# Row additions of two layer norms and the closing addition as accumulating transfers, with the closing norm in place

## The chip, the cores and the metric

The kernel runs on one core of a Trainium2 chip. The engines of the core are PE (matrix products), DVE (vector), ACT (activations), POOL (GpSimd) and SP, which here only issues transfers; each runs its own instructions in order and waits on semaphores for the others. The metric is the device time of one execution in microseconds.

## The reference, cut to what matters

The input x has 8 batches of 2048 nodes with 256 features; adj is a 2048 x 2048 mask. Two graph layers follow one another, each with a residual and a layer norm around it. Layer 0 is an attention over chunks of 256 nodes with four heads of 64:

```
scores = clip(q k / 8, -10, 10); where adj == 0: -10
attn   = softmax(scores) within each chunk of 256 nodes
ctx    = sum over the 8 chunks of attn v
out    = layernorm(ctx Wo + bo + x) * gamma + beta
x1     = layernorm(x + out)
```

Layer 1 is a graph attention on x1, again with four heads:

```
Wh    = x1 W
e     = leaky_relu(s_src + s_dst), masked by adj
alpha = softmax(e)
h     = elu(alpha Wh)
result = layernorm(x1 + h)
```

## The kernel before, in words

Everything is in float32 but the masks. The 2048 nodes of a batch are cut into four groups of 512 (four tiles of 128 rows). The loop over batches b runs layer 0 of batch b, and beside it layer 1 of batch b-1, and the closing norm of batch b-2. Layer 0 has 64 slots (4 groups of queries x 2 pairs of heads x 8 chunks), taken as 32 pairs; the loop `for p in range(PAIRS)` (L1104) emits one pair. With q = p // 8 and i = p % 8, pair p belongs to group q.

In each pair PE makes the scores `ps` (L398) of the next pair in four units, DVE clips them into `pr` (L415), ACT takes exponents in place (L438), PE multiplies with the values into `pc` (L449), ACT copies `pc` to `raw` (L456), DVE takes the reciprocal of the row sums (L466), and POOL scales and adds to `acc` (L473, L475). Beside it, `along` is layer 1 of the batch before: DVE makes four tiles `e` per pair from a row, a column and the mask `et` (L842), and PE multiplies each into `pa` (L871). When a head of layer 1 is done for eight tiles of rows, `close` (L891) divides, applies the elu and writes the result into `h1` in its last step on DVE (L915). The first such write of a batch falls into pair 6 and fills one head of rows 0 to 7 of `h1`.

All engines follow an order written out by hand: what is emitted first stands first in the queue of its engine. Transfers are issued by SP (loads, stores) and ACT (stores of `acc` and of x1). What stands in the list `outgoing` is sent at the start of the next pair by `send` (L205).

The work between the layers is done for one group at a time by class `Between` (L573), in steps that are hooked into the pairs by tables. For group q-1 during group q: `xg` is loaded at i=0 (L579), `bias` adds bo at i=2 (L584), PE makes the output projection `po` at the ends of i=2 and 3, `add` (L611) forms y at the starts of i=3 and 4, ACT takes sums and squares at the ends of i=4 and 5, `shift` (L588) adds beta - bo to `xg` at i=6, and ACT applies the norm at the end of i=6. In the group after that, `scale` (L617) multiplies with gamma at i=0, `again` (L620) adds `xg` at i=1, and the second norm follows: sums at the end of i=1, squares at i=2, then the apply and the store of x1. The last group of a batch is done between the batches by the list `steps` (L1232), and the last-but-one finishes at the last pair (L1187) and in the list `early`; these call the same methods.

The closing norm of batch b-2 is class `Close` (L930) driven by the table `CLOSING` (L1055): for each group g it loads x1 from `x1D` into `x1g` (L943), adds it to `h1` on DVE (L946), lets ACT take sums and squares, and writes the normed rows into `x1g` (L951), from which SP stores them (L952). Batches 6 and 7 have their closing norm after the loop over pairs, by the tables `CLOSING_ALONE` and `ENDING`; there POOL does the addition and the rows go through free space in `kT` and `qT`.

Of the kernel before, what the change touches and what calls it, by code (L numbers as in the profile page):

```python
# [8 lines left out]
F32 = mybir.dt.float32  # L9
# [4 lines left out]
ALU = mybir.AluOpType  # L14
AX = mybir.AxisListType

P = 128
# [4 lines left out]
def adj_resnorm_kernel(  # L22
# [19 lines left out]
    nc = tc.nc  # L42
    B, N, F = x.shape
    H, D = a_src.shape
    NT = N // P
    NCH = N // CH
# [8 lines left out]
    QT = CH // P  # L55
# [32 lines left out]
    blocks = ctx.enter_context(tc.tile_pool(name="blocks", bufs=2))  # L88
# [30 lines left out]
    qT = big.tile([P, KC, N], F32, tag="qT", name="qT")  # L119
    kT = big.tile([P, KC, N], F32, tag="kT", name="kT")  # L120
# [6 lines left out]
    x1D = tc.dram_tile([B, N, F], F32, name="x1D")  # L127
# [18 lines left out]
    def row(ap, name):  # L146
        t = consts.tile([P, F], F32, tag=name, name=name)
        nc.scalar.dma_start(out=t, in_=ap.partition_broadcast(P))
        return t
# [8 lines left out]
    bo_sb = row(bo, "bo_sb")  # L158
    gamma_sb = row(gamma, "gamma_sb")
    beta_sb = row(beta, "beta_sb")  # L160
# [44 lines left out]
    def send():  # L205
        while outgoing:
            outgoing.pop(0)()


    class Masks:  # L210
# [3 lines left out]
        def __init__(self):  # L214
            self.pieces = [
                (QT * q + u, m) for q in range(NCH) for m in range(len(PIECES)) for u in range(QT)
            ]
            self.raw, self.bits, self.done = [], [], []
            self.next = 0
# [47 lines left out]
    def by_node(dram, b, g):  # L267

        return dram[b, g * CH : (g + 1) * CH, :].rearrange("(t p) f -> p t f", p=P)
# [45 lines left out]
    def project(b, g):  # L315
# [18 lines left out]
        def linear(dst, w, bias, apart=False):  # L334
            if apart:
                pps = [one_bank([P, CH], "pp") for _ in range(KC)]
            else:
                pp = two_banks([P, KC, CH], "pp")
                pps = [pp[:, c, :] for c in range(KC)]
            for c in range(KC):  # L340
                for kc in range(KC):
                    nc.tensor.matmul(  # L342
                        pps[c],
                        lhsT=w[:, kc, c * P : (c + 1) * P],
                        rhs=st["xT"][:, kc, :],
                        start=(kc == 0),
                        stop=(kc == KC - 1),
                    )
            for c in range(KC):
                nc.scalar.activation(  # L350
                    dst[:, c, cols], pps[c], AF.Identity, bias=bias[:, c : c + 1]
                )
# [83 lines left out]
    def exps(s, u):  # L436
        pr = probs[s][u]
        nc.scalar.activation(pr, pr, AF.Exp, scale=0.125)  # L438
# [38 lines left out]
    sums = {}  # L477
# [95 lines left out]
    class Between:  # L573
# [5 lines left out]
            self.r = load_x(b, g, "xg")  # L579
            self.y = blocks.tile([P, QT, F], F32, tag="y", name="y")  # L580

        def bias(self):
            row = bo_sb.unsqueeze(1).to_broadcast([P, QT, F])
            nc.vector.tensor_add(self.r, self.r, row)  # L584

        def shift(self):
            row = beta_sb.unsqueeze(1).to_broadcast([P, QT, F])
            nc.vector.tensor_add(self.r, self.r, row)  # L588

        def output(self, us, parts=HALVES):  # L590
            n = len(us)
# [17 lines left out]
        def add(self, us):  # L609
            here = slice(us[0], us[0] + len(us))  # L610
            nc.vector.tensor_add(self.y[:, here, :], self.po, self.r[:, here, :])  # L611
            if us[0] == 0:
                self.a = Norm(self.y, "a")
# [2 lines left out]
            row = gamma_sb.unsqueeze(1).to_broadcast([P, QT, F])  # L616
            nc.vector.tensor_mul(self.y, self.y, row)  # L617

        def again(self):
            nc.vector.tensor_add(self.y, self.y, self.r)  # L620
            self.b2 = Norm(self.y, "b")

        def finish(self):
# [38 lines left out]
        4: lambda o: o.add((2, 3)),  # L662
    }
    MIDDLE_OF = {
        2: lambda o: o.bias(),
        6: lambda o: (o.a.factors(), o.shift()),
    }
    FINALLY_OF = {
        4: lambda o: o.a.sums(every),
# [6 lines left out]
    }  # L676
    NEXT_MIDDLE = {
        0: lambda o: o.scale(),
        1: lambda o: o.again(),
        3: lambda o: o.b2.factors(),  # L680
        4: lambda o: o.load(),
        5: lambda o: o.turn(),
# [4 lines left out]
        3: lambda o: o.finish(),  # L687
    }
    NEXT_LAST = {
        5: lambda o: o.values((0, 1)),  # L690
        6: lambda o: o.values((2, 3)),
    }
# [237 lines left out]
    class Close:  # L930


        def __init__(self, b, g, home):
            self.b, self.g = b, g
            self.h = h1[:, QT * g : QT * (g + 1), :]
            if len(home) == 3:
                pool, tag, bufs = home
                self.x = pool.tile([P, QT, F], F32, tag=tag, name="x1g", bufs=bufs)
            else:
                room, k = home  # L940
                at = k % 2 * QT * F
                self.x = room[:, k // 2, at : at + QT * F].rearrange("p (t f) -> p t f", f=F)
            nc.sync.dma_start(out=self.x, in_=by_node(x1D, b, g))  # L943

        def add(self, engine=nc.vector):
            engine.tensor_add(self.h, self.h, self.x)  # L946
            self.n = Norm(self.h, "c")

        def finish(self):
# [38 lines left out]
                else:  # L988
                    nc.scalar.activation(dst, src, AF.Identity, bias=off, scale=rs)

    HOME = (blocks, "xb", 2)
    HOME_Y = (blocks, "y", 2)

    class Closing:

# [4 lines left out]
        def do(self, s, *kinds):  # L1000
            for g, step, *more in self.table.get(s, ()):
                if step not in kinds:
                    continue
                if step == "load":
                    self.of[g] = Close(self.b, g, more if len(more) > 1 else more[0])
                elif step == "finish":
                    self.of[g].finish()
                elif step == "add":
                    self.of[g].add()
                elif step == "pool":  # L1010
                    self.of[g].add(nc.gpsimd)
                elif step == "stats":
                    self.of[g].n.stats((0, 1, 2, 3))
                elif step == "most":
                    self.of[g].add_most()
                elif step == "sums":
                    self.of[g].n.sums((0, 1, 2, 3))
                elif step == "squares":
                    self.of[g].n.squares((0, 1, 2, 3))
                elif step == "factors":  # L1020
                    self.of[g].n.factors()
# [9 lines left out]
    for g in range(NCH):  # L1031
# [21 lines left out]
            finish_constants()  # L1053

    CLOSING = {  # L1055
        -1: [(0, "load", HOME), (1, "load", HOME)],
        0: [(0, "add"), (0, "sums")],
        1: [(0, "squares")],
        2: [(1, "add"), (0, "factors"), (0, "finish"), (2, "load", HOME_Y)],
        3: [(1, "sums")],  # L1060
        4: [(1, "squares"), (3, "load", HOME_Y)],
        5: [(2, "add"), (1, "factors"), (1, "finish")],
        6: [(2, "sums")],
        7: [(2, "squares")],
        8: [(3, "add"), (2, "factors"), (2, "finish")],
        9: [(3, "sums")],
        10: [(3, "squares")],
        11: [(3, "factors"), (3, "finish")],
    }
    CLOSING_ALONE = {  # L1070
        -1: [(g, "load", kT, g) for g in range(NCH)],
        1: [(0, "pool")],
        2: [(1, "pool")],
        3: [(0, "stats")],
        4: [(1, "stats")],
        5: [(0, "finish")],
        6: [(1, "finish")],
        8: [(2, "pool")],
        9: [(3, "pool")],
        10: [(2, "stats")],  # L1080
        11: [(3, "stats")],
        12: [(2, "finish")],
        13: [(3, "finish")],
    }
    ENDING = {
        30: [(g, "load", qT, g) for g in range(NCH)],
        37: [(0, "pool")],
        38: [(1, "pool")],
        39: [(0, "stats")],
        40: [(1, "stats")],  # L1090
        41: [(0, "finish")],
# [5 lines left out]
    for b in range(B):  # L1097
        waug = blocks.tile([P, NT, H, D1], F32, tag="waug", name="waug")
        sd = small.tile([P, 2 * H, NT], F32, tag="sd", name="sd", bufs=1)
        closing = Closing(b - 2, CLOSING) if b > 1 else None  # L1100
        if closing:
            closing.do(-1, "load")
        group = before = None
        for p in range(PAIRS):  # L1104
            s0, s1 = 2 * p, 2 * p + 1
# [2 lines left out]
            more = p + 1 < PAIRS  # L1108

            def hook(now, later):  # L1110
                if group and i in now:
                    now[i](group)
                if before and i in later:
                    later[i](before)
# [78 lines left out]
            if along and more:  # L1193
                exps(*us[3])
            hook(LAST_OF, NEXT_LAST)
            hook(FINALLY_OF, NEXT_FINALLY)
# [55 lines left out]
        else:  # L1252

            step = lower.step
# [16 lines left out]
    closing, ending = Closing(B - 2, CLOSING_ALONE), Closing(B - 1, ENDING)  # L1271
# [3 lines left out]
    for s in range(SLOTS):  # L1275
        send()
        lower.step()
        for each in (closing, ending):
            each.do(s, "load", "pool", "stats", "most", "finish")
    send()  # L1280
    ends = [ending.of[2 + k].last(pa) for k, pa in enumerate(lower.pa)]
    for _ in range(3):
# [44 lines left out]
```

## Time and profile before

| | |
|---|---|
| median of 3 runs | 3737.82 us (3729.38 to 3747.32) |
| profiled execution | 3730.24 us, span 3728.4 us |
| PE, DVE, ACT, POOL busy | 95%, 82%, 62%, 39% of the span |
| TensorE clock granted | 0.99 |
| L620 y<-y,xg | 32 of 1423 ns mean |
| L588, L584 xg<-xg,row | 32 each of 1219 and 1207 ns |
| L946 h<-h,x1g on DVE | 24 of 1218 ns |
| transfers | queues of SP (47.3% of the 16 engines' span) and ACT (2.8%), none of POOL |

A line of the groups gives the line of the kernel, engine, operation, what is written from what, shape, count, busy time in us, mean ns of one, and the idle time of the engine ahead of it with what ended most of it. A line of the timeline or the chain gives the start and the duration in us.

### The profile page before, as it was taken

What the parts mean: (1) busy time and instruction counts of PE and PEld (TensorE: products, weight loads), DVE (VectorE), ACT (ScalarE), POOL (GpSimd) and SP (SyncE); (2) the same over time, 40 slices, a digit from 0 to 9 for tenths busy, and PEclk for the clock granted to TensorE, in tenths of its full rate; (3) what the DMA queues carried; (4) which work ended last, traced back from release to release, by engine and by line L of the source; (5) the groups of instructions that cost most, each with busy time, mean ns of one, the idle gap of its engine ahead of it and who ended that gap; (6) DMA issues with size and microseconds to landing.
All of it is one profiled execution on the core that took longest, in us unless ns stands there. A gap on an engine that the chain in (4) does not pass through costs nothing.

```text
span 3728.4 us, 169513 instructions
## 1 busy us (share of the span) xinstructions
PE 3549.5 (95%) x76884; PEld 2633.8 (71%) x76884; DVE 3057.6 (82%) x3652; ACT 2305.0 (62%) x4119; POOL 1462.6 (39%) x1259
## 2 busy tenths in 40 slices
PE   8999999999999999999999999999999999998766
PEld 5666677776777677776777767777667776775666
DVE  5886689868899698996999869987789969896877
ACT  4786456656666566665666656666566656666366
POOL 1554234333333344342433433433333333334366
PEclk9999999999999999999999999999999999999889
DMA  7754344545555454554545545555445545552575
GB/s 188 174 127 92 104 141 144 142 117 152 158 147 145 103 161 145 151 141 117 168 146 147 129 127 155 149 148 125 141 143 148 147 101 169 147 155 62 183 233 194
DMA packets 699779, 537.51 MB, mean 144 GB/s; under 512 B 430384, under 2 KB 529072, under 8 KB 699056
## 3 DMA queue, kind: packets, MB, share of 16 engines
q1 hardware_dynamic: 649056, 492.97, 47.3%
q10 hardware_dynamic: 50000, 33.70, 2.8%
q8 instruction: 601, 9.85, 1.1%
q14 instruction: 122, 1.00, 0.1%
HBM read 465.44 MB, written 61.08 MB: 141 GB/s over the span
## 4 chain that ended last, share of the span: by engine, by line
PE 64%; DVE 15%; issue 4%; DMA 3%; ACT 2%; POOL 1%; SPq 0%; DVEq 0%; ACTq 0%; POOLq 0%
PE pa L871 18%; PE pc L449 18%; PE ps L398 16%; DVE pr L415 6%; DVE e L842 5%; PE pp L342 4%; PE pw L642 3%; PE po L600 3%; PE pv L358 2%; DMA et<-edgeD 2%; DVE h L915 1%; DVE qT L493 1%; DVE y L620 0%; DVE xg L588 0%; ACT raw L456 0%
## 5 line engine op out<-in xcount | busy, mean ns | idle before, releaser
L438 ACT ACTIVATE pr<-pr 128x1024 f32<-128x1024 f32 x960 | 995.7, 1055 | 451.1 <-DVE pr L415 383.3
L415 DVE SCALAR_TENSOR_TENSOR pr<-ps,slab 128x1024 f32<-128x1024 f32 x960 | 1116.8, 1205 | 127.4 <-PE ps L398 103.7
L871 PEld LDWEIGHTS pa<-waug,e 128*64 128x64 f32 x32768 | 1019.3, 140 | 260.5 <-issue 203.6
L842 DVE SCALAR_TENSOR_TENSOR e<-srow,gd,et 128x1024 f32<-128x1024 f32 x896 | 1176.4, 1345 | 21.6 <-PE pa L871 8.8
L871 PE MATMUL pa<-waug,e 128*64 128x65 f32 x32768 | 1075.3, 225 | 79.3 <-DVE e L842 41.9
L449 PE MATMUL pc<-vaug,pr 128*64 128x65 f32 x30720 | 991.5, 222 | 42.3 <-DVE pr L415 24.6
L449 PEld LDWEIGHTS pc<-vaug,pr 128*64 128x64 f32 x30720 | 942.6, 138 | 70.8 <-DVE pr L415 42.5
L398 PE MATMUL ps<-qT,kT 64*64 64x512 f32 x8192 | 949.7, 597 | 13.7 <-DVE pr L415 11.1
L473 POOL TENSOR_TENSOR part<-raw,rd 128x512 f32<-128x512 f32 x448 | 474.0, 1058 | 1222.7 <-DVE rd L466 1219.0
L398 PEld LDWEIGHTS ps<-qT,kT 64*64 64x64 f32 x8192 | 285.6, 132 | 499.5 <-issue 271.2
L456 ACT COPY raw<-pc 128x520 f32<-128x520 f32 x512 | 303.0, 592 | 524.7 <-PE pc L449 523.3
L475 POOL TENSOR_TENSOR acc<-acc,part 128x512 f32<-128x512 f32 x448 | 595.6, 1329 | 35.1
L466 DVE RECIPROCAL rd<-raw 128x8 f32<-128x8 f32 x512 | 100.0, 195 | 188.9 <-ACT raw L456 185.3
L473 POOL TENSOR_TENSOR acc<-raw,rd 128x512 f32<-128x512 f32 x64 | 67.0, 1046 | 358.1 <-DVE rd L466 358.1
L642 PE MATMUL pw<-w_sb,x1T 128*64 128x264 f32 (+1 forms) x800 | 125.1, 392 | 7.5 <-DVE x1T L300 5.0
L600 PE MATMUL po<-wo_sb,qT 128*64 128x256 f32 (+1 forms) x912 | 120.2, 380 | 1.6 <-DVE rd L466 0.8
L342 PE MATMUL pp<-xT,wk_sb 128*128 128x512 f32 x256 | 118.5, 606 | 2.5 <-DVE xT L312 1.3
L358 PE MATMUL pv<-wv_sb,xT 128*128 128x256 f32 x512 | 119.1, 386 | 0.0
L816 POOL TENSOR_TENSOR e<-e,et 128x1024 f32<-128x1024 f32 x42 | 90.9, 2167 | 70.7 <-DMA et<-edgeD 31.7
L907 ACT ACTIVATE sums<-sums,dn 128x64 f32<-128x64 f32 x448 | 117.3, 336 | 0.5 <-DVE e L842 0.5
L842 DVE SCALAR_TENSOR_TENSOR e<-rowp,gd,et 128x1024 f32<-128x1024 f32 x86 | 104.9, 1272 | 15.2 <-DMA et<-edgeD 15.2
L342 PE MATMUL pp<-xT,wq_sb 128*128 128x512 f32 x256 | 115.9, 595 | 0.0
(140 smaller groups left out, 2550.5 us busy)
## 6 DMA issues: line engine op xcount, KB each, us to landing
et<-edgeD SPq DMA_DIRECT2D x896, 256.0 KB, 3.3
slab<-clipD SPq DMA_DIRECT2D x256, 256.0 KB, 4.2
srow<-rowD SPq DMA_DIRECT2D x64, 512.0 KB, 5.0
et<-edgeD SPq DMA_DIRECT2D x64, 512.0 KB, 5.3
xg<-in_x_dram SPq DMA_DIRECT2D x32, 512.0 KB, 5.6
x1D<-y ACTq DMA_DIRECT2D x32, 512.0 KB, 3.0
ctxD<-acc ACTq DMA_DIRECT2D x56, 256.0 KB, 3.7
ctx<-ctxD SPq DMA_DIRECT2D x224, 64.0 KB, 3.8
```

The lines of the kernel that those rows point to most:

```text
L342: nc.tensor.matmul(pps[c], lhsT=w[:, kc, c * P : (c + 1) * P], rhs=st["xT"][:, kc, :], start=(kc == 0), stop=(kc == KC - 1),)
L398: nc.tensor.matmul(ps[z * D : (z + 1) * D, k, :], lhsT=kT[rows, hp, t * P + z * D : t * P + (z + 1) * D], rhs=qT[rows, hp, cols], start=Tr ...
L415: nc.vector.scalar_tensor_tensor(pr, ps, -CLIP, row.unsqueeze(1).to_broadcast([P, 2, CH]), op0=ALU.max, op1=ALU.min,)
L438: nc.scalar.activation(pr, pr, AF.Exp, scale=0.125)
L449: nc.tensor.matmul(pc[z * D : (z + 1) * D, k, to], lhsT=probs[s][u][:, k, i * P + z * D : i * P + (z + 1) * D], rhs=vaug[:, KT * c + u, 2 ...
L456: nc.scalar.copy(raws[s].rearrange("p k i d -> p k (i d)"), pc[:, :, : QT * D1])
L473: nc.gpsimd.tensor_mul(part, raw[:, :, :, :D], rd.to_broadcast([P, 2, QT, D]))
L475: nc.gpsimd.tensor_add(accv, accv, part)
L600: nc.tensor.matmul(po[z, k, :], lhsT=qT[:, c, t * P + z.start : t * P + z.stop], rhs=wo_sb[:, c, :], start=(c == 0), stop=(c == KC - 1),)
L642: nc.tensor.matmul(pw[z, k, : F + 2 * H], lhsT=self.x1T[:, c, u * P + z.start : u * P + z.stop], rhs=w1_sb[:, c, :], start=(c == 0), stop= ...
L842: nc.vector.scalar_tensor_tensor(e, row, self.gd[:, h, j : j + 1], self.mask(k), op0=ALU.max, op1=ALU.mult,)
L871: nc.tensor.matmul(self.pa[i // QT][z * D : (z + 1) * D, i % QT, :], lhsT=e[:, i * P + z * D : i * P + (z + 1) * D], rhs=self.waug[:, j, h ...
```

## The change

`bias` and `shift` get a second form in which POOL issues a transfer that adds a row, repeated four times, into `xg`. The tables use it, one pair earlier than the additions of before: `bias` at i=1, `shift` at i=5. `again` likewise has a form in which a transfer adds `xg` into y; it is emitted at the end of i=0 of the group after, where before DVE added at i=1. The calls between the batches and at the last pair keep the additions on DVE.

In the closing norm of batches 0 to 5 x1 is no longer loaded into a tile of its own: POOL issues a transfer that reads `x1D` and adds into `h1`. The first two are issued at the start of the batch, the third at pair 5 behind the factors of group 1, the fourth at pair 7. The norm is applied in place in `h1`, and the store reads `h1`. The closing norms after the loop over pairs still load x1 into `kT` and `qT` and add on POOL.

```diff
+        def add_row(self, row, by_dma):
+            row = row.unsqueeze(1).to_broadcast([P, QT, F])
+            if by_dma:
+                nc.gpsimd.dma_start(out=self.r, in_=row, accum_op=ALU.add)
+            else:
+                nc.vector.tensor_add(self.r, self.r, row)
...
-        def again(self):
-            nc.vector.tensor_add(self.y, self.y, self.r)
+        def again(self, by_dma=False):
+            if by_dma:
+                nc.gpsimd.dma_start(out=self.y, in_=self.r, accum_op=ALU.add)
+            else:
+                nc.vector.tensor_add(self.y, self.y, self.r)
...
     MIDDLE_OF = {
-        2: lambda o: o.bias(),
-        6: lambda o: (o.a.factors(), o.shift()),
+        1: lambda o: o.bias(True),
+        5: lambda o: o.shift(True),
+        6: lambda o: o.a.factors(),
...
     NEXT_MIDDLE = {
-        1: lambda o: o.again(),
...
     NEXT_LAST = {
+        0: lambda o: o.again(True),
...
     class Close:
-        def __init__(self, b, g, home):
+        def __init__(self, b, g, room=None):
             self.b, self.g = b, g
             self.h = h1[:, QT * g : QT * (g + 1), :]
+            if room is None:
+                self.x = self.h
+                return
...
+        def add(self):
+            if self.x is self.h:
+                src = by_node(x1D, self.b, self.g)
+                nc.gpsimd.dma_start(out=self.h, in_=src, accum_op=ALU.add)
             else:
+                nc.gpsimd.tensor_add(self.h, self.h, self.x)
             self.n = Norm(self.h, "c")
...
     CLOSING = {
-        -1: [(0, "load", HOME), (1, "load", HOME)],
-        0: [(0, "add"), (0, "sums")],
+        -1: [(g, "load") for g in range(NCH)] + [(0, "add"), (1, "add")],
+        0: [(0, "sums")],
         1: [(0, "squares")],
-        2: [(1, "add"), (0, "factors"), (0, "finish"), (2, "load", HOME_Y)],
+        2: [(0, "factors"), (0, "finish")],
         3: [(1, "sums")],
-        4: [(1, "squares"), (3, "load", HOME_Y)],
-        5: [(2, "add"), (1, "factors"), (1, "finish")],
+        4: [(1, "squares")],
+        5: [(1, "factors"), (1, "finish"), (2, "add")],
         6: [(2, "sums")],
-        7: [(2, "squares")],
-        8: [(3, "add"), (2, "factors"), (2, "finish")],
+        7: [(2, "squares"), (3, "add")],
+        8: [(2, "factors"), (2, "finish")],
```

## The prediction

> **What bounds the kernel now.** I read the page first: the shares of busy time and the chain that ended last.
>
> ```profile
> PE 3549.5 (95%) x76884; PEld 2633.8 (71%) x76884; DVE 3057.6 (82%) x3652; ACT 2305.0 (62%) x4119; POOL 1462.6 (39%) x1259
> ```
>
> PE leads and DVE is second. An average cannot say whether 110 us less DVE work is worth anything, so I went to the chain in order of time. A pair of slots in the steady part of batch 3 reads:
>
> ```profile
> 1396.27 1.08 PE pa L871 x32
> 1397.35 1.87 PE pc L449 x64
> 1399.22 2.80 PE pa L871 x96
> 1402.02 1.87 PE pc L449 x64
> 1403.88 3.59 PE ps L398 x32
> ```
>
> That is 11.21 us of PE with no gap: the floor of a pair. Pairs with an output projection have 1.73 us more, those with the layer-1 values about 2 us. What stands above the floor is all that the change can win. I then asked for the busy times of stretches cut at the end of every second copy raw<-pc, that is pair by pair. In batch 4 the pairs 0, 2, 6, 7 and 14 read (columns: length, PE, PEld, DVE, ACT, POOL, clock, DMA share, GB/s):
>
> ```profile
> core 0: us, PE busy (x) PEld busy (x) DVE busy (x) ACT busy (x) POOL busy (x), PEclk, DMA share, GB/s
> 1743.60:1755.60 12.00, 10.10 (x280) 8.35 (x276) 12.00 (x13) 6.62 (x9) 1.04 (x1) 1.00 0.51 169
> 1766.90:1779.70 12.80, 11.44 (x292) 8.79 (x288) 12.40 (x14) 7.37 (x15) 6.86 (x6) 1.00 0.57 167
> 1814.80:1826.90 12.10, 11.53 (x292) 8.57 (x288) 12.10 (x14) 7.15 (x12) 4.66 (x4) 1.00 0.50 155
> 1826.90:1838.10 11.20, 11.20 (x292) 8.63 (x288) 10.05 (x11) 7.55 (x17) 4.66 (x4) 1.00 0.39 121
> 1911.60:1923.50 11.90, 11.41 (x292) 8.75 (x288) 11.90 (x16) 7.38 (x15) 6.80 (x6) 1.00 0.39 114
> ```
>
> The reader should see that pair 7 is on PE's floor with 1.1 us of DVE idle, while pairs 0, 6 and 14 have DVE busy for their whole length. So DVE is the bound exactly in pairs that carry an extra DVE instruction of 1.2 us, and PE everywhere else. Summed over pairs 1 to 31 the excess over the floor is about 10 to 15 us per batch (batches 1 to 6), of which 4 to 11 us are PE idle. With 73 us in those six batches this caps the gain at about 2% of the run.
>
> **What the skill says.** Two places bear. First, the Trainium skill's page "SBUF — State Buffer", section "Who interferes with whom", says that a DVE instruction with two SBUF inputs and a GpSimd instruction that reads SBUF shut each other out. The trace agrees: two e (L842) take 2.47 us at 1744.89 with POOL idle, and 3.56 us at 1812.64 with POOL's acc beside them. Hence a tensor_add that leaves DVE also takes a collision partner from POOL. I count nothing extra for that. Second, "DMA: Bandwidth & Descriptors", section "SWDGE vs HWDGE vs iDMA", says that accumulating transfers can only be issued from GpSimd, whose cores write the descriptors in software. No row of before shows such a transfer: its queues are those of SP and ACT alone.
>
> **The change part by part.** The DVE additions stand in these groups:
>
> ```profile
> L620 DVE TENSOR_TENSOR y<-y,xg 128x1024 f32<-128x1024 f32 x32 | 45.5, 1423 | 0.5
> L588 DVE TENSOR_TENSOR xg<-xg,beta_sb 128x1024 f32<-128x1024 f32 x32 | 39.0, 1219 | 0.2
> L584 DVE TENSOR_TENSOR xg<-xg,bo_sb 128x1024 f32<-128x1024 f32 x32 | 38.6, 1207 | 0.0
> L946 DVE TENSOR_TENSOR h<-h,x1g 128x1024 f32<-128x1024 f32 x24 | 29.2, 1218 | 0.0
> ```
>
> By the tables bias and shift go to transfers for three of the four groups of a batch (24 each of 32), again for two (16 of 32; the others run from the code at the last pair and between the batches, by DVE as before), the closing addition in all 24 places. DVE loses 24x1.207 + 24x1.219 + 16x1.423 + 24x1.218 = 110 us. POOL gains 88 issues. CLOSING_ALONE and ENDING keep their POOL additions. In POOL's queue each transfer stands ahead of the normalization (part, acc) of the same pair; in pair 5 the third add is queued behind the factors of group 1, so the closing apply doesn't wait for it. bias and shift are issued a pair earlier than DVE ran them, again half a pair, the fourth add one pair.
>
> *What the relief is worth.* Excess over the floor, mean of batches 2 to 6, and what I take of it: pair 0 (first closing add) 0.8, take 0.8; pairs 2 and 3 (second add) 2.0, take 1.2, the length of the add; pairs 8 to 10 (fourth add, bias of pair 10) 2.1, take 1.2, since part is a late et load behind SP's wait for the closing apply, which stays; pairs 14 and 15 (shift) 1.2, take 1.0; pair 17 (again) 0.3, take 0.1, since DVE is only just full there; pair 18 (bias) 0.5, take 0.5; pairs 22 and 30 (shift) 0.7 and 0.4, take 0.3 each; pairs 25 and 26 (again, bias) 0.9, take 0.6. Sum 6.0 us per batch. The third add (pair 5) comes below. Batches 2 to 6 give 5x6.0 = 30; batch 7 loses the last 1.2 because its layer-1 work ends at pair 23, so 4.8; batch 1, without closing, 3.1; batch 0, where only pairs 10, 14, 17 and 18 show PE idle (0.3 to 0.7), 1.5. In all 39 us gained.
>
> *What "in place" costs.* Before, the norm's result went to x1g, and h1 was free once ACT had read it. Now the result stands in h1 until its output transfer has landed. Look at pair 6 of batch 4 and the transfer's landing time:
>
> ```profile
> 1815.70 2.07 ACT L564 ACTIVATE x1g<-h,off_c,rs_c 128x256 f32<-128x256 f32 x4
> 1817.79 0.39 SPq L952 DMA_DIRECT2D out_dram<-x1g  x1
> 1818.46 0.95 DVE L915 SCALAR_TENSOR_TENSOR h<-ee,sums 128x512 f32<-128x512 f32 x1
> 1819.33 2.47 DVE L842 SCALAR_TENSOR_TENSOR e<-srow,gd,et 128x1024 f32<-128x1024 f32 x2
> ```
> ```profile
> out_dram<-x1g SPq DMA_DIRECT2D x24, 512.0 KB, 3.3
> ```
>
> L915 writes the first head of the next batch's rows 0 to 7 of h1, and group 1 is rows 4 to 7. It starts 0.0 to 0.7 us after the issue of group 1's output in all six batches, so it has to wait for the landing: 3.3 - 0.4 = 2.9 us. Behind it on DVE stand two e, a transpose of the context (0.70), a reciprocal and two pr. The second product of the pair needs the first of these pr to free its bank; in this trace that pr ended near 1823.6 and the product began at 1824.13, only 0.55 us later. So about 2.4 us reach PE, in a pair where DVE was already 12.1 of 12.1 us. What the third add saves in pair 5 (at most 1.2 us) is swallowed, as the landing hangs on ACT's apply, which follows the end of pair 5. Six batches: 6x2.5 = 15 us lost. Other writes of h1 (pair 10 on, rows 8 to 15 from pair 22 on) come over 20 us after the output that they must follow.
>
> *What the new transfers cost.* POOL's issue: at least SP's 0.43 us for a 512 KB load, at most some 5 us if the software writes its 512 pieces of 1 KB slowly. POOL has 6.5 us free in a pair (11.2 less 4.66), and raw has two buffers, so POOL may run some 9 us late before ACT waits: nothing at either end; beyond 6.5 us it is paid. Landing: the plain x1g load of the same size took 3.1 to 7.3 us; with the target read as well I take 8, between 4 and 15. Room until the consumer: bias 1.5 pairs (17 us), shift to again 33 us, second and third closing add 14 us or more, first closing add about 14 us (POOL ends waug at 1739.5, ACT sums at 1756.4), again about 12 us (issued behind the normalization of the last part of a pair, read by ACT's sums at the end of the next). Only again is near, and costs 0 at 8 us. The SP queue loses the x1g loads (0.4 us each): nothing. DMA engines: bias falls into pairs 9, 17 and 25, where SP also issues four ctx loads and the DMA share is 0.64 to 0.69. An et load lands in 3.4 us and is issued about three uses (8.4 us) ahead, so it has 5 us to spare, less in pair 9. I take 9 us in all, between 0 and 50.
>
> *Sum.* -39 + 15 + 9 = -15 us: 3730 (the profiled execution: span 3728.4, 3730.24 with what lies around) becomes 3715. The median of the runs is 3737.8, 8 above it, so I forecast 3723, with a range of its own of 3710 to 3735. About 0.5% (19 us) is what a measurement here can tell from no change, as the three runs spread over 18 us.
>
> **The rivals.**
> (1) The wait on the landing costs nothing, because the lead of two e and the three PSUM banks cover it. For: DVE idles 1.1 us in pair 7 and could catch up. Against: the 0.55 us of slack at the second product. Then -39 + 9 = -30: 3708.
> (2) The slower side: DMA engines. If an accumulating transfer reads source and target, it is 1.05 MB for the engines. In pair 17 they moved 191 GB/s at a share of 0.67, so 285 KB per us when busy: 3.7 us of all engines each. again and bias follow one another in pairs 16 and 17 (and 24 and 25), 7.4 us in a stretch of 22 with 7.3 idle. It decides once et lands more than 5 us late. With 2.5 us of PE at pairs 9, 17 and 25 in seven batches, +52: 3723 + 52 = 3775. For it: DVE already waits for et 15 times (20.6 us), and the chain has such a transfer at pairs 9 and 10 of every batch from 2 on. Against: two x1g loads at the start of a batch run beside et loads, and no e waits there.
> (3) again lands later than 12 us, or POOL is held over 6.5 us per issue, and ACT waits. At 1 us for each of the 16 again, the gain shrinks to nothing: 3738. For: nothing in the trace bounds either. Against: the plain load's 7.3 us at most.
>
> **How the numbers follow.** Forecast 0.42, rival 1 0.15, rival 2 0.31, rival 3 0.12. Faster by over 0.5% (below 3719): 0.13 of the forecast's share, 0.14 of rival 1, 0.01 of rival 3, 0.28. Within: 0.29 + 0.01 + 0.04 + 0.06 = 0.40. Slower: 0.27 + 0.05 = 0.32. The range reaches from just below rival 1 to rival 2: 3702 to 3775.
>
> **What would show it.** Right: pairs 0, 2, 14 and 18 at 11.2 to 11.4 us with DVE idle; L915 of pair 6 released by the output transfer from h, waiting 2 to 3 us, and pair 6 at 13.5 us or more. Wrong: DVE or PE waiting for et in pairs 9, 17, 25 (rival 2); ACT's sums waiting for y or h by transfer (rival 3); L915 without a wait (rival 1). The prediction fails most easily on the unknown price of the accumulating transfer, on POOL and on the DMA engines.

## The result and the profile after

The changed kernel takes 3784.1 us (median of 4 runs, 3781.1 to 3786.4) against 3733.6 us before in the same session: a ratio of 1.013 (95% interval 1.0113 to 1.0147), about 49 us slower. Its profiled execution has a span of 3779.3 us.

DVE did lose its work, and yet PE has a smaller share of a longer span. The page of the changed kernel: the busy times, the queue of the new transfers (packets, MB, share of the 16 engines' span), and the shares of the chain that ended last, by engine. The last line is the same chain in the kernel before.

```profile
PE 3559.0 (94%) x76884; PEld 2645.3 (70%) x76884; DVE 2954.6 (78%) x3564; ACT 2303.7 (61%) x4119; POOL 1540.2 (41%) x1347
q0 software_dynamic: 40320, 46.14, 8.1%
PE 77%; DVE 4%; issue 4%; DMA 2%; ACT 1%; POOL 1%; SPq 0%; DVEq 0%; ACTq 0%; POOLq 0%
```
```profile
PE 64%; DVE 15%; issue 4%; DMA 3%; ACT 2%; POOL 1%; SPq 0%; DVEq 0%; ACTq 0%; POOLq 0%
```

DVE went from 3057.6 to 2954.6 us, and its share of the chain from 15% to 4%. The price of a transfer stands in the groups and in the issues of the changed kernel (POOL's time per issue; then KB and median us from issue to landing):

```profile
L591 POOL DMA_DIRECT2D xg<-bo_sb x24 | 32.0, 1333 | 0.0
L626 POOL DMA_DIRECT2D y<-xg x16 | 14.9, 931 | 0.0
```
```profile
xg<-bo_sb POOLq DMA_DIRECT2D x24, 512.0 KB, 7.9
xg<-beta_sb POOLq DMA_DIRECT2D x24, 512.0 KB, 7.8
h<-x1D POOLq DMA_DIRECT2D x24, 512.0 KB, 8.3
y<-xg POOLq DMA_DIRECT2D x16, 512.0 KB, 5.7
```

POOL pays 0.9 to 1.4 us an issue and a transfer lands in 6 to 8 us. Both are inside what the prediction allowed, and nobody who consumes these transfers waits for them. The loss is elsewhere. Pairs 6, 13, 14 and 17 of batch 3 of the changed kernel, cut as in the prediction:

```profile
1373.20:1387.30 14.10, 12.12 (x292) 8.82 (x288) 11.63 (x14) 7.19 (x12) 4.65 (x4) 1.00 0.56 148
1468.80:1483.20 14.40, 11.41 (x292) 8.79 (x288) 10.07 (x10) 9.06 (x21) 5.92 (x5) 1.00 0.90 216
1483.20:1494.40 11.20, 11.20 (x292) 8.67 (x288) 10.89 (x14) 7.38 (x16) 5.83 (x6) 1.00 0.23 70
1517.00:1530.80 13.80, 11.40 (x292) 8.79 (x288) 10.31 (x11) 7.36 (x13) 5.91 (x5) 1.00 1.00 239
```

Pair 14, where DVE did shift before, is now on PE's floor of 11.2 us. Pairs 13 and 17, where the transfers of shift and bias run, have no engine that is busy for their length: PE misses 3.0 and 2.4 us, DVE idles 4.3 and 3.5 us. What is full there is the last column but one, the share of the DMA engines: 0.90 and 1.00. Over batches 2 to 6 the excess over PE's floor at the pairs of the row transfers (9, 13, 17, 21, 25, 29) rose from 1.7 to 8.2 us per batch, and at pairs 6 and 7 from 1.3 to 4.7 us.

Two different waits lie behind this. The first is the one at pair 6 (timeline of the changed kernel; the bracket gives the idle time of the engine and what ended it):

```profile
1376.19 0.39 SPq L963 DMA_DIRECT2D out_dram<-h  x1
1379.61 0.69 DVE L924 SCALAR_TENSOR_TENSOR h<-ee,sums 128x512 f32<-128x512 f32 x1 [2.47 <-DMA out_dram<-h]
1380.21 2.48 DVE L851 SCALAR_TENSOR_TENSOR e<-srow,gd,et 128x1024 f32<-128x1024 f32 x2
```

The write of h1 waits for the store that reads it, 2.47 us of DVE idle here and 20.7 us in six such waits. The second was not foreseen. The chain through pair 17 of batch 3:

```profile
1522.81 2.80 PE pa L880 x96
1525.61 1.63 PE pc L449 x54
1527.23 2.40 issue
1529.63 0.51 PE pc L449 x9
1530.14 3.59 PE ps L398 x32
```

PE stops for 2.40 us in the middle of a group of 64 products, after the 54th. Within such a group there is nothing to wait for: all operands were there at its start. "issue" says that the profile shows no semaphore that PE waited on. The sums of such waits, before and after:

```profile
PE pc L449 <- issue: 17.3, 26, 1.6
DVE e L842 <- DMA et<-edgeD: 20.6, 15, 6.7
```
```profile
PE pc L449 <- issue: 56.6, 41, 3.0
DVE h L924 <- DMA out_dram<-h: 20.7, 6, 4.9
DVE e L851 <- DMA et<-edgeD: 37.5, 22, 5.1
```

**What PE waits for.** The page has, in both kernels, a queue of its own for instructions (packets, MB, share of the 16 engines' span):

```profile
q8 instruction: 601, 9.85, 1.1%
```

Its packets have 16,384 bytes each. PE executes 153,916 instructions (products, weight loads and its own waits). Shared over the 601 packets that is 256.1 instructions a packet, or 64 bytes an instruction. So these are PE's instructions, 256 to a packet, one packet every 6.2 us. The Trainium skill says the same on its page "Runtime: NRT & Kernel Launch", section "Instruction fetch mechanics": an engine's instruction memory is refilled in blocks of 16 KiB, that is 256 instructions, over a queue of the sequencer's own, and the cost of this is "mostly hidden". The trace agrees with the block; how well the cost is hidden depends on what else the DMA engines carry. Here is pair 17 of batch 3 again, from the packet records of the trace:

```
POOL's issue of xg<-bo_sb          1519.88 to 1521.20
packets of that transfer (528)     1521.77 to 1527.54, mean 0.111 us
fetch of PE's next 256 instr.      1527.21 to 1528.15
PE stops / goes on                 1527.23 / 1529.63
```

The fetch itself takes 0.94 us (the median of all 601 is 0.98 us); it began only as the accumulating transfer ended. I took two measures from the records. A stall is put down to a fetch if PE idles over 0.2 us and goes on 1.15 to 1.7 us after the end of a fetch (all 26 stalls inside pc groups in the trace of before end 1.26 to 1.72 us after one, where chance would put one stall in thirteen there). And a fetch is late if it begins over 4 us after the early point in PE's own instruction count at which fetches begin (the point that 2% of them undercut). The table runs from the first batch's end to pair 22 of batch 7 (late fetches and the last column, which is explained below: from 400 to 3400 us):

| | stalls after a fetch, us | late fetches | at half clock, us |
|---|---|---|---|
| before | 32 | 12 | 0 |
| changed | 79 | 50 | 27 |

Other ends of the stretch move the sums of stalls by up to 3 us, and another early point moves the counts of late fetches, but neither changes their order. Of the 79 us, 53 begin within 9 us of an issue by POOL.

That PE really runs out of instructions is seen from the count of them. If PE's instructions are numbered in order, then in the trace of the changed kernel (400 to 3400 us) all 51 stalls over 0.5 us that follow a fetch come after the same place of a block of 256, the 193rd; in the trace of before it is 25 of 26. The other stalls over 0.5 us, 21 in each trace, are spread over the block, with at most one at that place. A wait for data would have no reason to respect this count. The fetches that come early begin about 280 instructions ahead of the place where PE would stop. With 576 instructions in a pair of 11.2 us this is 5.4 us, and fetch and restart take 2.4 of them. So about 3 us of delay are covered, by an estimate from these numbers.

The last column is a cost beside the stalls. In the changed kernel the clock records show seven stretches, six of 3.4 us and one of 6.8, in which the granted clock was 0.50. The kernel before has none in this part. Each begins between 1.4 us before and 1.6 us after the end of an idle time of PE of 1.9 to 2.8 us. A product of pc takes 311 to 316 ns there, against 222 in the mean of before. PE's busy time is 9.5 us longer for the same 76,884 products; half of 27 would be 14. No run separates the lower clock from the idle time that it comes with.

The rise of the stalls, 47 us, is about as large as the loss. That alone proves nothing, as gains and other losses stand beside it; the experiments decide.

### The profile page after: what moved, and what is told of

Its sections match the earlier page's. It is cut to its first block, busy times and chain, and to the rows that moved or that the text cites. A ratio compares the mean times of both kernels' runs of the same rounds, so it can differ in the third digit from the quotient of the medians.

```text
span 3779.3 us, 169657 instructions
## 1 busy us (share of the span) xinstructions
PE 3559.0 (94%) x76884; PEld 2645.3 (70%) x76884; DVE 2954.6 (78%) x3564; ACT 2303.7 (61%) x4119; POOL 1540.2 (41%) x1347
## 3 DMA queue, kind: packets, MB, share of 16 engines
q14 instruction: 124, 1.01, 0.1%
## 4 chain that ended last, share of the span: by engine, by line
PE 77%; DVE 4%; issue 4%; DMA 2%; ACT 1%; POOL 1%; SPq 0%; DVEq 0%; ACTq 0%; POOLq 0%
PE pa L880 23%; PE pc L449 22%; PE ps L398 20%; PE pp L342 4%; PE pw L650 3%; PE po L605 3%; PE pv L358 2%; DVE pr L415 2%; DMA et<-edgeD 1%; DVE e L851 1%; DMA srow<-rowD 0%; DMA out_dram<-h 0%; ACT h L564 0%; ACT raw L456 0%; DVE st_c L516 0%
## 5 line engine op out<-in xcount | busy, mean ns | idle before, releaser
L398 PE MATMUL ps<-qT,kT 64*64 64x512 f32 x8192 | 957.4, 599 | 17.4 <-DVE pr L415 11.2
```

The costliest lines, as they stand in the source:

```text
L398: nc.tensor.matmul(ps[z * D : (z + 1) * D, k, :], lhsT=kT[rows, hp, t * P + z * D : t * P + (z + 1) * D], rhs=qT[rows, hp, cols], start=Tr ...
```

## The experiments

Theories: (F) PE's instruction fetches, and with them the et loads, are held up by the accumulating transfers; (W) the store of the closing norm holds up DVE's write of h1; (R) the relief of DVE is worth what the prediction said, or nothing. Ratios are to the kernel before on the same chip, with 95% intervals; a difference of two ratios times 3734 gives microseconds.

### The parts of the change

**own_out.** The closing norm's result goes to a tile of its own; all transfers stay.

```diff
             o = self.x
+            if o is self.h:
+                o = blocks.tile([P, QT, F], F32, tag="xb", name="x1g", bufs=2)
             self.n.apply(o)
```

> The changed kernel, but the closing norm writes its result to a tile of its own, so that the write of h1 in pair 6 need not wait for the output transfer. If that wait (20.7 us over six batches in the trace of the changed kernel) is what made it slower: 3784 - 20 = 3764 us, and pairs 6 and 7 back near 11.2 to 12.5 us. If PE's late instruction fetches beside the accumulating transfers made it slower: about 3780 or more, with the stalls in the middle of pc groups as many as before.

Measured 3762.0 us, 1.0072 (1.0043 to 1.01). The wait on out_dram<-h is gone from the list, and 0.0058 of the ratio with it: 22 us (give or take 12), W's share. The time is the one that was expected of W, and not the 3780 us of F. But the kernel is still 27 us slower than before, and PE's stalls inside pc groups are all there, so both are at work:

```profile
PE pc L449 <- issue: 63.8, 50, 3.2
DVE e L851 <- DMA et<-edgeD: 43.0, 21, 5.2
```

**rows_only.** The changed kernel with class Close, its tables and its calls as before:

```diff
-        -1: [(g, "load") for g in range(NCH)] + [(0, "add"), (1, "add")],
+        -1: [(0, "load", HOME), (1, "load", HOME)],
...
```

> Only the row additions and again are done by accumulating transfers (64 of them); the closing norm is that of the kernel before. Fetch theory: PE stalls in the middle of pc groups grow by about 34 us at pairs 9, 13, 17, 21, 25 and 29, less some 20 us of DVE relief: about 3748 us. If the wait for the output were the cause, this version has none and gains the relief: about 3714 us.

Measured 3765.1 us, 1.007 (1.0052 to 1.0088): 26 us slower with no wait for a store. It is dearer than F expected; that W alone is the cause is out.

**close_only.** The changed kernel with the tables of the rows as before:

```diff
-        1: lambda o: o.bias(True),
-        5: lambda o: o.shift(True),
-        6: lambda o: o.a.factors(),
+        2: lambda o: o.bias(),
+        6: lambda o: (o.a.factors(), o.shift()),
...
+        1: lambda o: o.again(),
...
-        0: lambda o: o.again(True),
```

> Only the closing addition is done by accumulating transfers (24) and its norm in place; the rows are added by DVE as before. Wait theory: +20 us for the wait less 12 us of relief, 3742 us. Fetch theory on top: about 15 us more at pairs 0, 5, 7 and 8: 3757 us.

Measured 3754.8 us, 1.0049 (1.0034 to 1.0064): 18 us slower, between the two expectations. The stalls after a fetch rose by 17 us. The two halves add up within the intervals: 0.0070 + 0.0049 = 0.0119 against 0.013.

**left_out.** The kernel before without the 88 DVE additions, nothing in their place.

```diff
     MIDDLE_OF = {
-        2: lambda o: o.bias(),
-        6: lambda o: (o.a.factors(), o.shift()),
+        6: lambda o: o.a.factors(),
...
-        1: lambda o: o.again(),
+        1: lambda o: o.second(),
...
-        def add(self, engine=nc.vector):
-            engine.tensor_add(self.h, self.h, self.x)
+        def add(self, engine=None):
+            if engine:
+                engine.tensor_add(self.h, self.h, self.x)
```

(`second` only makes the norm.)

> The kernel before with 88 of its DVE additions left out (24 bias, 24 shift, 16 again, 24 closing), no transfers in their place: part of the computation is missing, so this is the upper end of what relief of DVE is worth. By the prediction's sum -39 us: 3695 us. If DVE's relief is worth nothing because PE bounds: 3734 us.

Measured 3698.6 us, 0.9893 (0.9864 to 0.9922): relief is worth 40 us, as the prediction said. So the transfers of own_out, which has the same relief, cost 1.0072 - 0.9893 = 0.0179, or 67 us (give or take 15). Between these two traces the stalls after a fetch rise from 39 to 83 us, the time at half clock from 3 to 24 us, and DVE's waits for et from 19.7 to 43.0 us.

### What about a transfer is dear

The next four differ only in what stands at the 48 places of bias and shift in the pairs (i=1 and i=5); again and the closing norm are those of before.

```diff
     MIDDLE_OF = {
-        2: lambda o: o.bias(),
-        6: lambda o: (o.a.factors(), o.shift()),
+        1: lambda o: o.moved(bo_sb),
+        5: lambda o: o.moved(beta_sb),
+        6: lambda o: o.a.factors(),
```

In `moved` stands, for **pair_add**, **pair_copy_pool** and **pair_copy_sp** in this order:

```diff
+            nc.gpsimd.dma_start(out=self.r, in_=row, accum_op=ALU.add)
...
+            nc.gpsimd.dma_start(out=self.r, in_=row)
...
+            nc.sync.dma_start(out=self.r, in_=row)
```

**pair_none** has neither the additions nor the transfers.

> The kernel before with the 48 additions of bias and shift in the pairs left out and nothing in their place (part of the computation is missing). It is the base line for the next three. By the prediction's sum for these pairs, about 2.8 us per batch: 3734 - 20 = 3714 us.

> Bias and shift alone as 48 accumulating transfers, everything else as before. Fetch theory: the instruction fetches of PE wait until the accumulating transfer is through; about 40 us more than the version without these additions, so 3755 us. If the transfers cost nothing by themselves: 3714 us.

> The same 48 transfers in the same places from POOL's queue, but as plain copies that overwrite the target (the addition is left out). If any transfer from POOL's queue holds up the fetches: 3755 us as with accumulation. If it is the accumulation, by its slow packets (0.12 us a packet of 1 KB against about 0.04): 3715 to 3725 us.

> The same 48 plain copies issued by SP instead (the addition is left out). If only transfers from POOL's queue are harmful: 3714 to 3720 us. If 512 KB more on the engines is harmful whatever the queue, it is as the plain copies from POOL's queue.

| | median us | ratio (interval) | stalls after a fetch, us | late fetches | at half clock, us |
|---|---|---|---|---|---|
| pair_none | 3709.6 | 0.992 (0.99 to 0.994) | 39 | 22 | 3 |
| pair_copy_sp | 3709.9 | 0.9926 (0.9904 to 0.9947) | 41 | 24 | 0 |
| pair_copy_pool | 3732.9 | 0.999 (0.998 to 1.0) | 63 | 24 | 3 |
| pair_add | 3761.0 | 1.0057 (1.0037 to 1.0077) | 81 | 51 | 27 |

The same lines of the waits, pair_none first, then pair_add:

```profile
PE pc L449 <- issue: 22.3, 29, 2.0
DVE e L841 <- DMA et<-edgeD: 21.1, 16, 5.3
```
```profile
PE pc L449 <- issue: 61.0, 45, 3.0
DVE e L847 <- DMA et<-edgeD: 43.0, 24, 5.1
```

The same bytes to the same places cost nothing measurable as plain copies from SP's queue, 26 us as plain copies from POOL's, and 51 us as accumulating transfers from POOL's. That is 1.07 us for each of the 48, nearly the length of the DVE instruction that it replaced (1.2 us), and more than the 30 us that leaving out the 48 additions gained (pair_none). The 42 us more of stalls and the lower clock account for it. In the packet records the 48 accumulating transfers occupy 2851 us of engine time, 2851 / 48 / 16 = 3.7 us of all engines each, the plain copies from POOL's queue 1.9 us (1424 us in all). Why the plain copies from POOL cost more than those of SP is open: their packets are larger (4 KB against 1 KB), their stalls are more, but the count of late fetches is the same. The 3732.9 us lie between what was expected if the queue alone mattered (3755) and if accumulation alone did (3715 to 3725).

**pair_quarters.** As pair_add, but each transfer in four parts of one tile (128 KB), half a pair apart.

```diff
+        def quarter(self, row, k):
+            nc.gpsimd.dma_start(out=self.r[:, k, :], in_=row, accum_op=ALU.add)
...
     MIDDLE_OF = {
-        2: lambda o: o.bias(),
-        6: lambda o: (o.a.factors(), o.shift()),
+        1: lambda o: o.quarter(bo_sb, 0),
+        2: lambda o: o.quarter(bo_sb, 2),
+        5: lambda o: o.quarter(beta_sb, 1),
+        6: lambda o: (o.a.factors(), o.quarter(beta_sb, 3)),
...
     LAST_OF = {
-        2: lambda o: o.output((0, 1)),
+        1: lambda o: o.quarter(bo_sb, 1),
+        2: lambda o: (o.output((0, 1)), o.quarter(bo_sb, 3)),
         3: lambda o: o.output((2, 3)),
+        4: lambda o: o.quarter(beta_sb, 0),
+        5: lambda o: o.quarter(beta_sb, 2),
```

> Bias and shift as accumulating transfers as in the version with these alone (3761 us), but each in four parts of 128 KB that are issued half a pair apart: the same bytes, four times the issues. If a fetch has to wait until the transfer before it is through, it now waits 1.5 us at most instead of 5.8, which its lead can cover: 3715 to 3740 us. If it is the engines' load over all: 3761 us or more.

Measured 3723.0 us, 0.9983 (0.9972 to 0.9995). The bytes and the accumulation are those of pair_add, the issues are four times as many, and 28 of the 51 us are gone, with the stalls:

```profile
DVE e L850 <- DMA et<-edgeD: 24.5, 15, 6.1
PE pc L449 <- issue: 23.8, 31, 1.5
```

Stalls after a fetch are 44 us, late fetches 19, and 3 us are at half clock. So it is less the sum of the load on the engines that does the harm than the time for which one transfer holds them without a break. This is what F says: a fetch has a lead that covers a block of about 1.7 us and not one of 5.5 us (the mean spans of a transfer's packets in the two traces). The 24 us that remain over pair_none are not explained by 5 us more of stalls.

### Other ways to the relief

**pool_rows.** POOL adds instead of transferring.

```diff
+            nc.gpsimd.tensor_add(self.r, self.r, row)
```

> Bias and shift as POOL's own additions (2.35 us each by the trace of before) in the places of the transfers, no transfer added. DVE's relief without the fetch delays: 3710 us, plus what POOL's reads cost DVE (at most 1 us in 48 places): 3710 to 3740 us.

Measured 3731.5 us, 1.0 (0.9989 to 1.0011). The fetch stalls are those of the versions without transfers (38 us), but the relief is gone too. Its groups suggest why:

```profile
L847 DVE SCALAR_TENSOR_TENSOR e<-srow,gd,et 128x1024 f32<-128x1024 f32 x896 | 1252.8, 1430 | 18.7 <-PE pa L876 9.8
L588 POOL TENSOR_TENSOR xg<-xg,beta_sb 128x1024 f32<-128x1024 f32 x24 | 76.2, 3176 | 0.0
L588 POOL TENSOR_TENSOR xg<-xg,bo_sb 128x1024 f32<-128x1024 f32 x24 | 74.7, 3114 | 0.0
```

DVE's e went from 1345 to 1430 ns, 896 x 85 ns = 76 us more DVE work than before, against 58 us of additions taken off. This agrees with the rule on two SBUF inputs beside a GpSimd read that the prediction took from the skill.

**pool_all.** As pool_rows, and the closing additions on POOL, each behind the factors of the group before.

```diff
-        def add(self, engine=nc.vector):
+        def add(self, engine=nc.gpsimd):
...
-        2: [(1, "add"), (0, "factors"), (0, "finish"), (2, "load", HOME_Y)],
+        2: [(0, "factors"), (1, "add"), (0, "finish"), (2, "load", HOME_Y)],
...
```

> As the version before it, and the closing addition on POOL as well, with the closing norm's result in its own tile: no accumulating transfer and no wait for an output. Relief of the closing additions on top, about 12 us: 3700 to 3730 us.

Measured 3734.5 us, 1.0007 (0.9995 to 1.0019): no gain, a little above the expectation, with e at 1452 ns.

**parts_all.** Both causes met: all 88 transfers in parts, and own_out's tile.

```diff
+        def again_part(self, k):
+            nc.gpsimd.dma_start(out=self.y[:, k, :], in_=self.r[:, k, :], accum_op=ALU.add)
...
+        def add_part(self, k):
+            src = by_node(x1D, self.b, self.g)
+            nc.gpsimd.dma_start(out=self.h[:, k, :], in_=src[:, k, :], accum_op=ALU.add)
...
+        -1: [(g, "load") for g in range(NCH)] + [(0, "part", k) for k in range(QT)],
+        0: [(1, "part", 0), (0, "sums"), (1, "late", 1)],
+        1: [(1, "part", 2), (0, "squares"), (1, "late", 3)],
...
```

> All 88 additions as accumulating transfers, but each in four parts of 128 KB spread over the pairs (those of again two by two, those of the first closing group back to back), and the closing norm's result in a tile of its own. Both causes are met: 3699 us (nothing added, nothing computed) plus what 48 transfers in parts cost (3723 - 3710 = 13 us) times 88/48: 3722 us. If the closing and again transfers still hold up fetches because theirs stand closer together: 3730 to 3745 us.

Measured 3723.5 us, 0.9969 (0.9959 to 0.9978). This is the change with its two faults mended: 12 us faster than before, 1.6% faster than the change as it was made, and 0.0076 of the ratio (28 us) short of left_out. Stalls after a fetch are 50 us against 39 there, and DVE's e takes 1352 ns in the mean against 1329; how the 28 us split is open.

## Why the prediction was wrong

The forecast was 3723 us, the range 3702 to 3775; measured were 3784. Step by step, in us:

| step | predicted | measured |
|---|---|---|
| relief of DVE | -39 | -40 ± 11 (left_out) |
| wait for the store of the closing norm | +15 | +22 ± 12 (changed against own_out) |
| the new transfers | +9, between 0 and 50 | +67 ± 15 (own_out against left_out) |
| sum | -15 | +49 ± 6 |

(± is the 95% interval.) The three measured terms are the steps between four kernels, so they add up by construction.

**The relief was right**, and its way, pair by pair from the excess over PE's floor: in the changed kernel the excess of pairs 14 and 15 fell from 1.2 to 0.5, of pairs 2 and 3 from 2.0 to 1.2. One entry was badly founded: pair 0 had no pair before it in my cut and its length of 12 us was my own choice, so the 0.8 there measured nothing. By the distance from the last slot of a batch to the end of the next pair 0, left_out gains 0.5 to 1.5 us there, the changed kernel nothing (72.4 before, about 72.4 after).

**The wait was right** in place, instruction and releaser. It was undersized: 20.7 us in six waits are 3.5 us each where 2.9 were predicted, and the price of 22 us shows no slack that took any of it.

**The step that failed is "What the new transfers cost"**, its sentence on the DMA engines: 9 us. The engines' time was in the prediction, as rival 2's 3.7 us of all engines for a transfer, and was measured as 3.7. The step failed in who suffers. It looked for consumers among the loads that the kernel issues, gave et 5 us to spare, and so looked at pairs 9, 17 and 25 alone, where SP is busy too. The consumer it missed is not in the kernel's text: PE's instruction stream, one block every 6.2 us, which stood in the page of before as a queue with 601 packets. It is exposed at pairs 13, 21 and 29 too, at which the prediction did not look: the excess there rose by 1.0 us in the mean, and by 1.2 at 9, 17 and 25. In place of the 9 us the runs show 67: 44 more of stalls after a fetch, some 10 for the half clock (estimated as half of the 21 us more spent at it), and the rest, 13, is within the interval. DVE's longer waits for et are real (23 us more), but how much of them reaches PE was not separated.

**The rivals.** Rival 2 has the right sign and nearly the size (3775), from the engines' load. That it comes so near is in part luck: it put its 52 us on late et loads at three pairs of a batch alone, and pair_quarters shows that the unbroken block weighs more than the load. Rival 1 falls with own_out, rival 3 with the landings of 5.7 to 8.3 us: ACT waits for none of them. Nor does POOL come late for ACT: the waits of ACT's pr for acc are 63.1 us in the changed kernel and were 57.7 before.

What the runs leave open is how the engines choose between the queues, hence why the fetch gets its turn late; what the late et loads would cost by themselves, as the two delays were never separated; and whether the half clock comes from the stalls or only with them.

## What to carry to other kernels

A kernel whose bound engine runs many small instructions has one more stream to feed: count its instructions, find the queue that carries them, and ask of every large new transfer how long it can keep that stream waiting. If an accumulating transfer is wanted, cut it into parts and spread them; one block of 512 KB cost more here than leaving out the vector instruction gained. A result written in place is held by its store as long as by its readers: look for who writes the same rows next, and how soon.

## What the runs showed of the hardware that was not expected

- PE's instructions come as 601 packets of 16 KB for 153,916 instructions. In the changed kernel all 51 stalls over 0.5 us that followed a fetch came after the same place of a block of 256. PE went on 1.2 to 1.6 us after the end of the fetch, with few exceptions, and stalls inside a group of products, without any semaphore, reached 3.2 us (own_out).
- Between 400 and 3400 us the granted clock was 0.50 for 3.4 or 6.8 us beside some idle times of PE of 1.9 to 3.1 us: 24 to 31 us in all in the four kernels with whole accumulating transfers of the rows, 0 to 7 us in the ten others.
- 512 KB from SBUF to SBUF: 48 plain copies from SP's queue cost 2 us in all (within the interval), from POOL's 26 us, accumulating from POOL's 51 us. An accumulating transfer took 3.7 us of all 16 engines and 5.7 to 8.9 us to land, a plain one from POOL 1.9 and 5.4 to 5.7 us.
- A POOL addition of 128 x 1024 with a repeated row took 3.1 us beside DVE's work, against 1.2 us on DVE, and lengthened DVE's e from 1345 to 1430 ns in the mean.
